# Constant products on TensorE in front of and between the first attention steps, and the exponentials' table load behind the second squares

## Chip, cores and metric

One Trainium2 chip; the kernel runs on one of its cores. The metric is the device time of one execution in microseconds (us). A profile is one execution recorded by the hardware profiler; times within it count from the first instruction.

## The reference

Two pre-norm layers over 8 sequences of 256 tokens with 256 channels, all float32. Layer 0 is an attention without separate query, key and value weights, then a mixture of 4 experts (2 per token) with a shared expert. Layer 1 is an RWKV recurrence, then a mixture of 8 experts. What the change touches is the attention of layer 0, on the normalised input `x`:

```python
w = (x @ W.T).reshape(Bb, Tt, HEAD, DIM_HEAD).transpose(0, 2, 1, 3)   # 16 heads of 16
q, k, v = _rms_norm(w, g1), _rms_norm(w, g2), _rms_norm(w, g3)
att = jnp.einsum('bhid,bhjd->bhij', q, k) / sqrt_d
score = jax.nn.softmax(att, axis=-1) + jax.nn.softmax(att, axis=-2)
y = jnp.einsum('bhij,bhjd->bihd', score, v).reshape(Bb, Tt, C)
return y @ W
```

## The kernel before

All eight sequences stay in SBUF as tiles `xs[b]` (128 partitions, two halves of 128 tokens). Before the first branch the kernel loads them, builds constants (`ident`, `ones` and others by GpSimd), sets the activation table for square roots with a one-element activation on the tile `spare` (L1476), and normalises and transposes sequence 0 in a PSUM pool `p0` (L223 to L252, tile `xmT`). Then it branches on a bound of the gains; the branch taken here calls `layers(True)`, whose attention is `attention_bounded`.

The attention is a list of small functions for each sequence, placed by number into steps (`steps`, with `at(n, f, ...)`). Within a step they run in the order of the list `mine`. For sequence 0 the order is: step 0 `norm` (already there) and `project_in`; step 1 `scale`; step 2 `turn`; from step 3 on four steps of `exponentials`, with `values` one step behind. For sequence 1: `ready` in step 0, `norm` and `project_in` in step 1, `scale` in step 4, `turn` in step 5; sequence 2 has its `norm` in step 5.

- `ready` is the layer norm (VectorE, with a power on GpSimd, L216 and L217); `norm` transposes it on TensorE (L246) and copies it out on ScalarE (L252).
- `project_in` multiplies by the weights (L499: 4 products of 256 columns, each recorded as two passes), squares on ScalarE (L504), sums over a head on VectorE (L506). Sequence 0 then takes a square root on ScalarE (L509), runs an `Exp` of one element to fetch the exponentials' table (L510) and inverts on VectorE (L511); the other sequences use a power on GpSimd (L515), about 5.4 us long.
- `scale` multiplies by that factor on VectorE (L525). `turn` transposes on TensorE (L539), copies `kT` out on ScalarE (L541), makes `qT` on VectorE (L544) and has GpSimd copy `nv` (L547).
- `exponentials` makes the scores (L563: four strips of 32 rows side by side, 512 columns, two passes each, into four PSUM tiles `sc`), takes the exponential on ScalarE (L576, L568), sums (L577) and divides (L579, L580). `values` multiplies by the values (L594).

TensorE's order is the order in which this program text issues (`tc.manual_schedule(engines={ENG.PE})`). The orders of the other engines' queues are laid out at compile time by a planner from priorities and estimated times; it also picks the PSUM buffer for each tile of a tag. The tag `ps` has 4 buffers, the tag `sc` 4. `tc.issue_after(i)` queues what is issued under it behind `i` on the same engine.

## Time and profile before

| | us |
|---|---|
| median of 3 runs (lowest, highest) | 754.26 (754.13, 755.09) |
| the profiled execution | 760.07 |
| its span, first to last instruction | 757.7 |
| TensorE matmul busy in the span | 653.3 (86%) |
| VectorE busy | 462.9 (61%) |
| ScalarE busy | 358.8 (47%) |
| GpSimd busy | 244.5 (32%) |
| mean granted TensorE clock | 0.941 |

How to read the lines of a profile: a row of the timeline begins with its start in us, then the time from the start of its first to the end of its last instruction, the engine (PE is TensorE, PEld its weight loads, DVE VectorE, ACT ScalarE, POOL GpSimd), the line of the kernel, the operation, the tile written and the tiles read, and xN for N instructions. The bracket gives the idle time of the engine before it and what ended that. PEclk is the granted TensorE clock, 1.00 for the full one.

### The profile page before, as it was taken

The page shows a single profiled execution, that of the slowest core. Times are in us where ns is not written, and L with a number is a line of the kernel's source. Part 1 is how long each engine was busy: PE and PEld are TensorE (multiplying, and loading weights), DVE is VectorE, ACT ScalarE, POOL GpSimd, SP SyncE. Part 2 cuts the span into 40 slices and gives each one's busy share as a digit, 9 for nine tenths or more (in the row PEclk, how much of TensorE's full clock was granted, in tenths as well). Part 3 has the DMA queues.
Part 4 walks back from the last instruction along what each step waited for, and adds up shares of the span by engine and source line. Part 5 has one row for each costly group of instructions (what it writes and reads, how often), then busy time and mean ns, then how long its engine had stood idle before and what let it go on. Part 6 is the DMA issues. An engine that isn't in the chain of part 4 may idle for free. (4 is left out here: it accounts for less than half of the span.)

```text
span 757.7 us, 10756 instructions
## 1 busy us (share of the span) xinstructions
PE 653.3 (86%) x3170; PEld 417.3 (55%) x3170; DVE 462.9 (61%) x1216; ACT 358.8 (47%) x761; POOL 244.5 (32%) x319
## 2 busy tenths in 40 slices
PE   3799999996989999998899888986848989989790
PEld 2355555555765666665566656654735656554460
DVE  6699878897351111110866877673998895745542
ACT  3588767772213233322377467544147464423230
POOL 3434333300212333323222132112141446465430
PEclk9699999998999999999999999998879999999996
DMA  7800000001101111112300010002780445556844
GB/s 227 292 1 15 15 15 15 15 15 48 65 15 33 52 36 42 43 41 85 118 29 27 28 39 11 28 29 72 231 283 8 138 126 170 172 194 220 269 127 143
DMA packets 38547, 66.85 MB, mean 88 GB/s; under 512 B 6006, under 2 KB 20654, under 8 KB 38480
## 3 DMA queue, kind: packets, MB, share of 16 engines
q1 hardware_dynamic: 30400, 47.01, 18.9%
q0 software_dynamic: 7392, 18.50, 7.9%
q8 instruction: 31, 0.51, 0.3%
q10 hardware_dynamic: 688, 0.55, 0.2%
q14 instruction: 36, 0.29, 0.1%
HBM read 51.32 MB, written 16.41 MB: 89 GB/s over the span
## 5 line engine op out<-in xcount | busy, mean ns | idle before, releaser
L1002 POOL DMA_INDIRECT xg<-asked,source x77 | 78.4, 1018 | 186.5 <-PE ps L1012 164.1
L1050 POOL DMA_INDIRECT back<-yg,row_i x77 | 80.6, 1047 | 113.7 <-ACT yg L1049 35.3
L1041 DVE TENSOR_TENSOR h<-h,mm 128x512 f32<-128x512 f32 x37 | 25.3, 685 | 108.3 <-PE mm L1020 108.2
L1014 ACT COPY hT<-ps 128x256 f32<-128x256 f32 (+1 forms) x77 | 36.4, 473 | 95.8 <-PE ps L1012 87.2
L1020 PE MATMUL mm<-v1s,xgT 128*128 x160 | 76.9, 600 | 1.5 <-ACT xgT L1014 0.8
L576 ACT ACTIVATE e<-sc,minus 128x512 f32<-128x512 f32 x96 | 59.9, 711 | 28.5 <-PE sc L563 28.4
L1020 PE MATMUL mm<-w2s,hT 128*128 x296 | 72.0, 382 | 0.0
L1020 PE MATMUL mm<-w1s,xgT 128*128 x148 | 71.6, 602 | 0.2 <-ACT xgT L1014 0.2
L1020 PE MATMUL mm<-w3s,xgT 128*128 x148 | 70.7, 597 | 0.0
L577 DVE TENSOR_REDUCE s<-e 128x2 f32<-128x512 f32 x96 | 60.5, 677 | 13.3 <-ACT e L576 13.1
L563 PE MATMUL sc<-qT,kT 32*128 32x512 f32 x256 | 58.1, 703 | 2.9 <-DVE qT L544 2.2
L1020 PEld LDWEIGHTS mm<-w2s,hT 128*128 128x128 f32 x296 | 53.7, 191 | 7.1 <-issue 1.4
L1170 PE MATMUL sc<-mix,rw 128*128 128x256 f32 x192 | 49.3, 405 | 5.9 <-DVE mix L1159 4.2
L515 POOL TENSOR_TENSOR rr<-rr,minus_half 128x32 f32<-128x32 f32 x7 | 38.0, 5429 | 50.0 <-DVE rr L513 49.9
L1012 PEld LDWEIGHTS ps<-ident,h 128*128 128x128 f32 x228 | 28.8, 141 | 44.0 <-issue 27.7
L1020 PE MATMUL mm<-v2s,hT 128*128 x160 | 44.3, 396 | 3.1 <-ACT hT L1014 3.1
L216 POOL TENSOR_TENSOR rs<-mv,eps_ln 128x2 f32<-128x2 f32 x40 | 8.6, 215 | 118.4 <-DVE mv L211 75.6
L1012 PE MATMUL ps<-ident,h 128*128 128x128 f32 x228 | 39.4, 276 | 8.4 <-DVE h L1035 7.2
L1020 PEld LDWEIGHTS mm<-w3s,xgT 128*128 128x128 f32 x148 | 28.0, 193 | 33.9 <-issue 33.2
L1170 PEld LDWEIGHTS sc<-mix,rw 128*128 128x128 f32 x192 | 38.2, 205 | 14.2 <-DVE mix L1159 5.3
L1039 ACT ACTIVATE h<-mm 128x512 f32<-128x512 f32 x37 | 22.1, 598 | 43.1 <-PE mm L1020 43.1
L1032 DVE TENSOR_TENSOR hb<-mm,bias 128x512 f32<-128x512 f32 x40 | 27.5, 687 | 22.5 <-PE mm L1020 18.9
(246 smaller groups left out, 1254.2 us busy)
## 6 DMA issues: line engine op xcount, KB each, us to landing
bias<-bd SPq DMA_DIRECT2D x40, 384.0 KB
y<-back SPq DMA_DIRECT2D x16, 512.0 KB
asked<-xm SPq DMA_DIRECT2D x16, 256.0 KB
x<-in_x_dram SPq DMA_DIRECT2D x8, 256.0 KB
w1s<-in_w_dram SPq DMA_DIRECT2D x4, 512.0 KB
w3s<-in_w_dram SPq DMA_DIRECT2D x4, 512.0 KB
w2s<-in_w_dram SPq DMA_DIRECT2D x4, 512.0 KB
v1s<-in_v1g_dram SPq DMA_DIRECT2D x8, 256.0 KB
```

Source lines behind the costliest of these rows:

```text
L515: on_pool["last"] = nc.gpsimd.tensor_tensor(rr, rr, half, ALU.pow)
L563: nc.tensor.matmul(pa, lhsT=q["kT"][rows, u, ts(t, P)], rhs=q["qT"][rows, u], start=True, stop=True)
L576: nc.scalar.activation(e, pa, AF.Exp, bias=minus)
L577: nc.vector.tensor_reduce(q["s"][:, t, h : h + 2], e, AX.X, ALU.add)
L1002: nc.gpsimd.indirect_dma_start(out=xgs[j], out_offset=None, in_=self.asked, in_offset=bass.IndirectOffsetOnAxis(ap=self.source[:, j : j + ...
L1012: nc.tensor.transpose(pt[:, c, :], src[:, ts(c, P)], ident)
L1014: nc.scalar.copy(to, pt)
L1020: nc.tensor.matmul(po.unsqueeze(1), lhsT=lhsT[:, c, :], rhs=w[:, ds(e, 1), c, :], start=(c == 0), stop=(c == n - 1))
L1032: nc.vector.tensor_tensor(hb, ph, biases[j][:, 0 : 2 * I2], ALU.add)
L1041: nc.vector.tensor_tensor(s, s, pg, ALU.mult)
L1050: inst = nc.gpsimd.indirect_dma_start(out=self.back, out_offset=bass.IndirectOffsetOnAxis(ap=self.row[:, j : j + 1], axis=0), in_=yg, in_o ...
L1170: last = nc.tensor.matmul(po[:, o, :], lhsT=w[:, c, ts(o, P)], rhs=m[:, c, :], start=(c == 0), stop=(c == NC - 1))
```

## The change

Four edits.

1. In front of the transposes of sequence 0, TensorE multiplies the 128x128 tile `ones` by itself 34 times, into a PSUM tile `idle` that nobody reads.
2. A new function `keep(n)` does n such products into a tile of the tag `ps`. It is the last in its step: 3 products at the end of step 0, 5 at the end of step 1, 9 at the end of step 2.
3. The one-element `Exp` on `spare` leaves sequence 0 and is issued in `project_in` of sequence 1, queued behind its squares on ScalarE.
4. `keep` is added to the list that orders a step.

```diff
             n = ap2.tile([P, TT, NH, DH], F32, tag="n", name="n")
-            nc.scalar.activation(n, pw4, AF.Square)
+            square = nc.scalar.activation(n, pw4, AF.Square)
+            if b == 1:
+
+                with tc.issue_after(square.ins):
+                    nc.scalar.activation(spare, eps_rms, AF.Exp)
             rr = ap2.tile([P, TT, NH], F32, tag="rr", name="rr")
             nc.vector.tensor_reduce(rr, n, AX.X, ALU.add)
             if b in turned_in:
 
                 nc.scalar.activation(rr, rr, AF.Sqrt, bias=eps_rms, scale=1.0 / DH)
-                nc.scalar.activation(spare, eps_rms, AF.Exp)
                 nc.vector.reciprocal(rr, rr)
...
+        def keep(n):
+
+            idle = fresh()[0]([P, P])
+            for _ in range(n):
+                nc.tensor.matmul(idle, lhsT=ones, rhs=ones, start=True, stop=True)
+
...
-            mine = (ready, norm, exponentials, scale, turn, project_in, to_tokens, values, turn_back, project_heads, take_norm, fill)
+            for n, k in enumerate((3, 5, 9)):
+                at(n, keep, k)
+            mine = (ready, norm, exponentials, scale, turn, project_in, to_tokens, values, turn_back, project_heads, take_norm, fill, keep)
...
     with tc.tile_pool(name="p0", bufs=1, space=PSUM) as p0:
+
+        idle = p0.tile([P, P], F32, tag="idle", name="idle")
+        for _ in range(34):
+            nc.tensor.matmul(idle, lhsT=ones, rhs=ones, start=True, stop=True)
         xn = layer_norm(lnp, 0, "xm", bufs=3)
```

## Prediction

> **What bounds the kernel now.** I read the page first, then the chain of waits, then the timeline of each engine over the first 48 us, then the windows of 1 us over the same stretch. The page says that TensorE is the busiest engine and where its clock is low:

> ```profile
> PE 653.3 (86%) x3170; PEld 417.3 (55%) x3170; DVE 462.9 (61%) x1216; ACT 358.8 (47%) x761; POOL 244.5 (32%) x319
> PEclk9699999998999999999999999998879999999996
> ```

> The chain that ended last covers only the last 17 us (moves to `back` and `y`), which the change doesn't touch. So the question is by how much the change brings forward the attention, and whether all behind it follows. It should: from 38 us on TensorE is busy without a hole in nearly every slice, and nothing later waits for a fixed time (the first weights have landed by 36 us, where the DMA share falls to 0). I take a shift at 35 us as a shift of the end, one to one.

> TensorE in the timeline:

> ```profile
> 10.16 1.23 PE L246 MATMUL ps<-ident,xm 128*128 128x128 f32 x4 [10.16 <-DVE xm L223]
> 12.77 3.34 PE L499 MATMUL ps<-awt,xmT 128*128 128x256 f32 x8
> 15.94 0.60 PE L246 MATMUL ps<-ident,xn 128*128 128x128 f32 x4
> 17.33 1.99 PE L499 MATMUL ps<-awt,xnT 128*128 128x256 f32 x8 [0.79 <-ACT xnT L252]
> 20.50 0.63 PE L539 MATMUL ps<-ident,n 128*128 128x128 f32 x4 [1.17 <-DVE n L525]
> 23.33 2.09 PE L563 MATMUL sc<-qT,kT 32*128 32x512 f32 x8 [2.21 <-DVE qT L544]
> 30.22 1.94 PE L594 MATMUL ps<-e,nv 128*32 128x256 f32 x16
> ...
> 42.46 1.14 PE L563 MATMUL sc<-qT,kT 32*128 32x512 f32 x8
> ```

> The same eight passes cost 3.34 and 1.99 us, the same four transposes 1.23 and 0.60, a free set of scores 2.09 and 1.14. The windows give the clock beside them (the first number after the stretch is its length, the next TensorE's busy time; the third from the right is the clock):

> ```profile
> 22.00:23.00 1.00, 0.00 (x0) 0.00 (x0) 1.00 (x2) 1.00 (x1) 1.00 (x1) 0.75 1.02 351
> 23.00:24.00 1.00, 0.67 (x4) 0.55 (x8) 0.19 (x1) 0.04 (x1) 1.00 (x1) 0.50 1.05 388
> 29.00:30.00 1.00, 1.00 (x3) 0.00 (x0) 1.00 (x2) 1.00 (x2) 0.00 (x0) 0.50 1.08 363
> 36.00:37.00 1.00, 1.00 (x18) 0.42 (x16) 1.00 (x3) 1.00 (x3) 0.00 (x0) 0.92 0.00 0
> ```

> It falls to half at 22.75 and rises at 36.1. ScalarE and VectorE between the squares of sequence 0 and its first exponential:

> ```profile
> 12.10 1.28 ACT L510 ACT_TABLE_LOAD   x1
> ...
> 17.29 1.28 ACT L509 ACT_TABLE_LOAD   x1
> 18.59 0.32 ACT L509 ACTIVATE rr<-rr,eps_rms 128x32 f32<-128x32 f32 x1
> 21.16 0.59 ACT L541 COPY kT<-ps 128x512 f32<-128x512 f32 x1 [1.20 <-PE ps L539]
> 21.76 1.28 ACT L576 ACT_TABLE_LOAD   x1
> 25.41 1.84 ACT L576 ACTIVATE e<-sc,minus 128x512 f32<-128x512 f32 x3 [2.36 <-PE sc L563]
> ...
> 16.84 0.68 DVE L506 TENSOR_REDUCE rr<-n 128x32 f32<-128x512 f32 x1
> 19.29 0.34 DVE L511 RECIPROCAL rr<-rr 128x32 f32<-128x32 f32 x1
> ```

> The `Exp` on `spare` runs at 12.10, long before the root, so the root's table is fetched again on the path (17.29), and the exponentials' at 21.76.

> **The 34 products.** No row shows such a product. It is two passes of 128 columns. From the second L499 and L246 rows, 1536 more columns cost 1.39 us, 0.12 us per 128: 0.23 a product at the full clock; at the low one a 256-column pass is 3.34 / 8 = 0.42. `ones` is ready at 1.1. In the trace the clock rose about 3.8 us after 12.1, where TensorE became steadily busy; I bound the rise at 4.5 to 8.1 and take 6. Then 4.9 / 0.42 = 11.7 products run slowly and 22.3 take 5.1 us: the end is 11.1 (10.5 to 12.1). They delay the first transposes, which could start at 10.16. From there: transposes 0.60, copy 0.59, eight passes 1.86, squares 0.60, with gaps about 14.9, against 16.80 now. But the sum over heads (L506) stands at 16.84 behind VectorE's layer-norm statistics of later sequences, which run without a hole from 14.28. If the planner leaves that order, the products give nothing here and cost nothing; the cover is 1.9 us (an end at about 13.0), past which a delay counts in full.

> **3 and 5 products.** Behind the first eight passes (end 14.2) 3 cost 0.7; the transposes of sequence 1 then run 14.9 to 15.5, its copy to 16.1, its eight passes to 18.1, its squares to 18.75 (now 19.96). The 5 run to 19.3, just when `turn` can start; beyond that each 0.23 would count. Queued behind both is only this TensorE work.

> **The tables.** The fetch at 17.29 goes, since the table set at 2.21 stays: the root starts at 17.55, not 18.59. L511 could follow at 17.95, but VectorE now holds 1.77 us of other work between L506 and L511, about the load and the root (1.28 + 0.32) which the planner seems to have filled. Without the load it should place L511 about 1.0 earlier (bounds 0, same order, and 1.3). `scale` ends at 19.3, `turn` runs to 19.95. On ScalarE the moved `Exp` stands behind the second squares: 18.75 + 1.28 + 0.20 = 20.25, and the copy of `kT` is queued behind it, so that the copy starts at 20.25, not 21.16: 0.9 earlier, 0.3 lost to the load. `qT` follows the copy and ends at 22.3 (now 23.19).

> **9 products.** 2.1 us behind `turn`, to 22.0, inside the wait for `qT`. They should hold the clock over 22.75, and the scores at 22.4 take 1.14 instead of 2.09. First exponential at 23.55 instead of 25.41: **1.86 earlier**, 0.9 by the table and 0.95 by the clock.

> **What is late next.** Two steps of exponentials are bound by ScalarE (25.41 to 31.35) and shift whole. TensorE then needs a score set's last strip, L594, L246 and the next scores before ScalarE goes on at 35.24. Between 26.1 and 30.2 the strips run singly, so a quarter of the array works: the windows show TensorE busy at 29.00 with the clock still at 0.50 after four such microseconds. So I expect that the full clock is lost again in the same strips (around 25 to 27.5), that the dense part behind them starts slow as now, and that the whole shifts by 1.9 to 2.3. I take 2.3, as the clock falls later than it did and so a little of that part is quicker. [...]

> [...]

> **Sum.** Profiled execution 760.07, minus 2.3 is 757.8. The median of the runs is 5.8 below the profiled one; the shift is taken over unscaled: 754.26 - 2.3 = 752.0.

> **Rivals.**

> [...]

> *VectorE's order stays.* L511 stays at 19.29 and the tables give nothing; only the 0.95 of the scores is left: 753.3.

> *PSUM buffers.* `keep` takes buffers of `ps`. Were the four handed out in turn, the 5 products would wait for `scale` (19.3) and `turn` start at 20.5 as now, and the first L594 would wait for the second `scale`, now 32.5, then 31.3, against its start at 30.22: 1.1 later, 755.4. Against it: between `project_in` and `scale` of a later sequence five tiles of `ps` are taken in TensorE's order, which would lock up if they went in turn; so free ones are picked.

> *The products run slowly* (ends slower). If a stream of 128-column products doesn't raise the clock, 34 x 0.42 = 14.3 us end at 15.4. Transposes, copy, eight slow passes, squares and sum then end at 22.6, not 17.5: 5.1 later, less the 1.0 of the root: 758.4. It decides from 0.35 us a product on, where the cover of 1.9 us is used up. The eight passes that raised it at 15.9 speak against it.

> *The table isn't where the text wants it* (slower). The `Exp` is tied only behind the second squares, not behind the root. If the planner puts those squares ahead of the root, both tables are fetched again: squares 18.75, `Exp` 20.25, load 1.28, root at 21.5 instead of 18.59; the inverse 2.6 later than 19.29, less 0.95: 755.9. Against it, the sum that the root needs is ready 1.2 before those squares can run.

> **Chances.** Shift as summed 0.45 (own range 750.8 to 753.4); clock holds 0.18; order stays 0.20; PSUM 0.07; slow products 0.06; table 0.04. 0.2% is 1.5 us, about what a measurement of this kernel can tell from no change. Faster by more: 0.36 of the first, all of the second, 0.06 of the third, 0.60. Within: 0.09, 0.14, 0.05, 0.28. Slower: the last two and 0.02 of PSUM, 0.12. The range runs from half a microsecond below the second case (748.8) to the PSUM case (755.4) and leaves out the two slow ones.

> **What would show it.** Right: two table loads before 30 us instead of four, none ahead of L509; L511 near 18.3; the first L563 row near 1.14 at about 22.4; the first exponential near 23.5; a clock below 1 somewhere from 25 to 33. Wrong: a first L246 beyond 13; L511 still at 19.3; a wait of the second group of products for `n`; a clock of 1.00 throughout (then 5 us, not 2.3).

## The result and the profile after

The changed kernel takes 752.03 us in the median of 14 runs (748.36 to 756.06); the kernel before took 755.28 beside it (14 runs, 748.06 to 763.12). The ratio is 0.9953, with a 95% interval of [0.9932, 0.9975]: by it 3.5 us less, between 1.9 and 5.1 (the medians differ by 3.25). Forecast were 752.0 us and 2.3 less, from a time before of 754.26, the median of the 3 runs known then. The profiled execution took 750.92 with a span of 748.8.

From the page after:

```profile
PE 658.8 (88%) x3272; PEld 425.5 (57%) x3272; DVE 462.4 (62%) x1216; ACT 356.1 (48%) x759; POOL 244.6 (33%) x319
PEclk9999997998999999999999999999888999999995
```

The 102 new TensorE passes are there (34 + 17 products, two passes each), ScalarE has two table loads fewer, and the low clock of the second slice is gone; one in the seventh is new. TensorE in the timeline after (the lines of the kernel have moved by a few):

```profile
1.14 9.70 PE L1493 MATMUL idle<-ones 128*128 128x128 f32 x68 [1.14 <-POOL ones L126]
12.35 1.89 PE L499 MATMUL ps<-awt,xmT 128*128 128x256 f32 x8
16.02 1.99 PE L499 MATMUL ps<-awt,xnT 128*128 128x256 f32 x8 [0.68 <-ACT xnT L252]
20.41 0.63 PE L542 MATMUL ps<-ident,n 128*128 128x128 f32 x4 [1.28 <-DVE n L528]
20.87 2.17 PE L646 MATMUL ps<-ones 128*128 128x128 f32 x18
23.24 1.14 PE L566 MATMUL sc<-qT,kT 32*128 32x512 f32 x8 [0.20 <-DVE qT L547]
28.23 1.07 PE L597 MATMUL ps<-e,nv 128*32 128x256 f32 x16
```

The 34 products end at 10.84, and the projections, scores and value products shown here run at the full clock. But `turn` (L542) starts at 20.41, against 20.50 before: it still waits for VectorE's `n`. Why, ScalarE and VectorE show:

```profile
14.36 0.60 ACT L504 ACTIVATE n<-ps 128x512 f32<-128x512 f32 x1 [2.47 <-PE ps L499]
18.66 0.32 ACT L513 ACTIVATE rr<-rr,eps_rms 128x32 f32<-128x32 f32 x1 [2.69 <-DVE rr L510]
19.48 1.28 ACT L508 ACT_TABLE_LOAD   x1
21.07 0.59 ACT L544 COPY kT<-ps 128x512 f32<-128x512 f32 x1
24.37 1.84 ACT L579 ACTIVATE e<-sc,minus 128x512 f32<-128x512 f32 x3 [2.72 <-PE sc L566]
30.98 1.84 ACT L579 ACTIVATE e<-sc,minus 128x512 f32<-128x512 f32 x3 [0.41 <-PE sc L566]
...
17.05 0.72 DVE L223 TENSOR_SCALAR xn<-x,mv,rs 128x256 f32<-128x256 f32 x2
17.97 0.65 DVE L510 TENSOR_REDUCE rr<-n 128x32 f32<-128x512 f32 x1
19.20 0.34 DVE L514 RECIPROCAL rr<-rr 128x32 f32<-128x32 f32 x1
```

The squares of sequence 0 are ready at 14.96 (before: 16.80), and no load stands ahead of the root any more. But the sum that the root needs, at 16.84 before, is now at 17.97, behind 1.1 us of other VectorE work (the two `xn` of sequence 2 among it), so the root starts at 18.66 (before: 18.59) and the inverse at 19.20 (19.29). The copy of `kT` gains 0.09. What is gained comes from the clock: 0.95 in the first scores (1.14 against 2.09), and 3.2 more by the third set of exponentials, 30.98 against 35.24.

### The profile page after: what moved, and what is told of

Its sections match the earlier page's. It is cut to its first block, busy times and chain, and to the rows that moved or that the text cites. A ratio compares the mean times of both kernels' runs of the same rounds, so it can differ in the third digit from the quotient of the medians.

```text
span 748.8 us, 10957 instructions
## 1 busy us (share of the span) xinstructions
PE 658.8 (88%) x3272; PEld 425.5 (57%) x3272; DVE 462.4 (62%) x1216; ACT 356.1 (48%) x759; POOL 244.6 (33%) x319
## 3 DMA queue, kind: packets, MB, share of 16 engines
q1 hardware_dynamic: 30400, 47.01, 19.1%
## 5 line engine op out<-in xcount | busy, mean ns | idle before, releaser
L580 DVE TENSOR_REDUCE s<-e 128x2 f32<-128x512 f32 x96 | 60.5, 677 | 14.3 <-ACT e L579 14.1
L1181 PEld LDWEIGHTS sc<-mix,rw 128*128 128x128 f32 x192 | 37.2, 201 | 14.2 <-DVE mix L1170 5.7
L1031 PE MATMUL mm<-v2s,hT 128*128 x160 | 42.3, 383 | 1.0 <-ACT xgT L1025 0.5
L1050 ACT ACTIVATE h<-mm 128x512 f32<-128x512 f32 x37 | 22.1, 598 | 42.3 <-PE mm L1031 42.2
L1031 PEld LDWEIGHTS mm<-v1s,xgT 128*128 128x128 f32 x160 | 27.3, 190 | 21.5 <-issue 18.4
## 6 DMA issues: line engine op xcount, KB each, us to landing
w2s<-in_w_dram SPq DMA_DIRECT2D x4, 512.0 KB, 10.2
```

The source lines that it names most:

```text
L580: nc.vector.tensor_reduce(q["s"][:, t, h : h + 2], e, AX.X, ALU.add)
L1031: nc.tensor.matmul(po.unsqueeze(1), lhsT=lhsT[:, c, :], rhs=w[:, ds(e, 1), c, :], start=(c == 0), stop=(c == n - 1))
L1050: nc.scalar.activation(s, pu, AF.Silu)
L1181: last = nc.tensor.matmul(po[:, o, :], lhsT=w[:, c, ts(o, P)], rhs=m[:, c, :], start=(c == 0), stop=(c == NC - 1))
```

## Experiments

Runs of one kernel differ by several us, and the profiles show the clock's low stretches elsewhere in each. So each theory is read from the start of named instructions in the profiles, and the ratios serve as a check. The start of the first, third and last (32nd) set of exponentials, of the copy of `kT`, and the low clock between 20 and 160 us:

| kernel | kT | first | third | last | low clock from 20 to 160 us, at | ratio to before |
|---|---|---|---|---|---|---|
| before | 21.16 | 25.41 | 35.24 | 169.79 | 22.5 (13.7 long), 104.4 (3.4) | 1 |
| whole change | 21.07 | 24.37 | 30.98 | 169.75 | 76.7 (3.4), 100.6 (3.4), 117.7 (10.2) | 0.9953 [0.9932, 0.9975] |
| after_again | 21.16 | 24.46 | 34.21 | 169.55 | 27.4 (6.8), 99.1, 123.0, 140.0 (3.4 each) | 0.9946 [0.9917, 0.9975] |
| table_alone | 21.24 | 25.50 | 35.32 | 173.03 | 21.9 (13.7), 100.4, 124.3 (3.4 each), 141.3 (10.2) | 1.0023 [0.9987, 1.0059] |
| products_alone | 21.11 | 24.41 | 31.01 | 170.17 | 43.8, 77.9, 101.8, 118.9, 142.8 (3.4 each), 159.9 | 0.9973 [0.9943, 1.0002] |
| nine_alone | 21.34 | 24.64 | 31.25 | 171.45 | 61.3, 78.4, 102.3 (3.4 each), 119.4 (10.2) | 0.9952 [0.9922, 0.9981] |
| no_front | 21.67 | 24.96 | 33.14 | 172.18 | 28.9, 63.0, 80.1, 104.0, 121.0, 144.9 (3.4 each) | 1.0001 [0.9967, 1.0034] |
| sum_first | 20.42 | 23.84 | 30.44 | 169.70 | 60.4, 77.4, 101.3, 118.4, 142.3 (3.4 each), 159.4 | 0.9953 [0.9923, 0.9982] |
| strip_fill_alone | 21.12 | 25.37 | 36.23 | 169.14 | 22.1 (13.7) | 0.9952 [0.992, 0.9983] |
| strip_fill | 20.40 | 23.81 | 30.42 | 163.53 | none | 0.988 [0.9836, 0.9925] |
| strip_fill_again (the kernel of strip_fill) | 21.16 | 24.57 | 34.02 | 168.50 | 27.8 (6.8), 79.0 (3.4) | 0.99 [0.9864, 0.9937] |
| nine_strip | 21.42 | 24.73 | 31.33 | 164.17 | none | 0.9907 [0.9873, 0.9942] |

**The whole change once more** (no edit).

> The changed kernel once more, for a second profile. Clock theory (the products keep the full clock from the first scores to the dense part at 28 to 35 us): the exponentials that began at 35.24 before and at 30.98 after begin near 31, with a clock of 1.00 from 23 to 36. Rival, the summed shift of the prediction (full clock only for the first scores, lost in the strips): near 33, with a clock of 0.50 somewhere from 25 to 33.

Here the clock fell, where the summed prediction had it. TensorE in this profile, and the windows of both profiles of the changed kernel, first the whole change's and then this one's:

```profile
25.20 4.06 PE L566 MATMUL sc<-qT,kT 32*128 32x512 f32 x8 [0.73 <-ACT e L579]
29.19 1.93 PE L597 MATMUL ps<-e,nv 128*32 128x256 f32 x16
32.10 2.09 PE L566 MATMUL sc<-qT,kT 32*128 32x512 f32 x8
```

```profile
23.90:27.30 3.40, 2.67 (x15) 1.00 (x8) 2.01 (x4) 2.93 (x8) 2.72 (x1) 1.00 1.06 376
27.30:30.70 3.40, 3.40 (x31) 1.32 (x30) 3.08 (x8) 3.06 (x8) 0.00 (x0) 1.00 1.07 372
```

```profile
23.90:27.30 3.40, 2.67 (x15) 0.91 (x7) 1.92 (x4) 2.84 (x8) 2.80 (x1) 1.00 1.06 369
27.30:30.70 3.40, 3.40 (x19) 0.98 (x18) 2.63 (x7) 2.67 (x7) 0.00 (x0) 0.51 1.07 371
```

With the same busy time in the same stretch the clock held once and fell once. The third set starts at 34.21, 1.03 earlier than before instead of 4.26. So both of the cases that the prediction kept apart occur, with one and the same kernel. Of the six profiles with the 9 products and no strip products (whole change, after_again, products_alone, nine_alone, no_front, sum_first) the clock held here in four and fell in two.

What differs between them can be read from the table. Within one profile the changes of the clock lie whole multiples of 3.41 us apart (the starts in the row of products_alone: 34.1, 23.9, 17.1, 23.9 and 17.1; the changes at 22.51, 36.16, 104.43 and 107.84 before: 13.65, 68.27 and 3.41), and where this grid lies against the program differs between the two executions of the changed kernel (falls at 76.7 and 27.4, 14.4 times 3.41 apart). The stretches above are windows of the grid of after_again; on that of the whole change's profile the windows run from 22.1 to 25.5 and from 25.5 to 28.9, so they cut the single strips (25.11 to 28.23) at another place. In all nine profiles with the 9 products (the six, and three below with strip products) the outcome goes with that place: the clock fell in the three where a window begins within 0.5 us of the first exponential, and held in the six where the nearest begins 0.87 to 1.65 us before it or 1.13 behind it.

**The table alone.**

```diff
-        for _ in range(34): ...          # the products in front
-            for n, k in enumerate((3, 5, 9)): at(n, keep, k)
```

> Only the moved Exp, none of the products. Clock theory: the table gives nothing, since the planner puts the sum over heads behind more of VectorE's statistics (its order for this kernel has the sum behind the two xn of sequence 2, two aggregates and one more statistic): root near 18.7, first scores at 23.2 to 23.6 taking 2.09, the third set of exponentials at 35 to 35.5, time within 1 us of before. Rival, the prediction's sum: 0.9 earlier at kT and everything behind it, the third set near 34.3, about 753.4 against 754.3.

The copy of `kT` starts at 21.24, the scores take 2.09, the third set starts at 35.32: nothing is gained, as the clock theory has it. VectorE in this kernel:

```profile
16.77 0.72 DVE L223 TENSOR_SCALAR xn<-x,mv,rs 128x256 f32<-128x256 f32 x2
18.30 0.67 DVE L510 TENSOR_REDUCE rr<-n 128x32 f32<-128x512 f32 x1
19.35 0.35 DVE L514 RECIPROCAL rr<-rr 128x32 f32<-128x32 f32 x1
```

The sum stands 1.46 later than before, behind more of the statistics: the move of the `Exp` is what puts it back, without a single product.

**The products alone.**

```diff
-            if b == 1:
-                with tc.issue_after(square.ins): nc.scalar.activation(spare, eps_rms, AF.Exp)
...
                 nc.scalar.activation(rr, rr, AF.Sqrt, bias=eps_rms, scale=1.0 / DH)
+                nc.scalar.activation(spare, eps_rms, AF.Exp)
```

> All products, but the Exp left where it was. Clock theory: as the whole change: table loads at about 12 and 17 us and again before the first exponential, first scores near 23.2 taking 1.14, first exponential near 24.4, third set near 31, time that of the whole change within 1 us. Rival, the prediction's sum: 0.9 later than the whole change at every step, with the third set 0.9 behind it.

```profile
16.57 1.28 ACT L509 ACT_TABLE_LOAD   x1
17.87 0.32 ACT L509 ACTIVATE rr<-rr,eps_rms 128x32 f32<-128x32 f32 x1
24.41 1.84 ACT L576 ACTIVATE e<-sc,minus 128x512 f32<-128x512 f32 x3 [1.42 <-PE sc L563]
```

With the old order (sum at 16.80) the load is back ahead of the root, and yet the first exponential starts at 24.41, within 0.04 of the whole change. The load had cover here: ScalarE fetches it at 16.57 while VectorE is at the sum, and the inverse stands at 19.23 behind VectorE's statistics in any case. Together with table_alone: at these starts the table edit is worth nothing and the products all of it. The ratio, 0.9973, doesn't tell this kernel from the whole change, nor quite from before.

**The 9 alone.**

```diff
-            for n, k in enumerate((3, 5, 9)):
-                at(n, keep, k)
+            at(2, keep, 9)
...                                        # and neither the 34 nor the moved Exp
```

> Only the 9 products behind the first turn, nothing else of the change. Theory (what counts is the clock held into the first scores; the 34, the 3 and the 5 stand where VectorE's queue sets the pace): root at 18.6, kT near 21.1, first scores near 23.3 taking 1.14, first exponential near 24.4, as with all products; the third set at 31 or, where the clock falls in the strips, near 34. Time between 751 and 755 beside 757 to 758 before. Rival (the 34 and the 5 are needed to keep the clock up): low clock at about 22.5 as before, scores taking 2.09, first exponential at 25.4, no gain.

Scores at 23.51 taking 1.14, first exponential 24.64, third set 31.25, ratio 0.9952: nine products carry the gain of the change within 0.3 us at these points. The first set of passes is slow again (3.62 us), which costs no more than that.

**All but the 34.**

```diff
-        for _ in range(34): ...          # the products in front; all else of the change stays
```

> The whole change without the 34 products. Theory: the first products of sequence 0 run slowly again (about 3 us), but the sum over heads stands behind VectorE's other work at about 18.0 and nothing behind it moves: kT near 21.1, first exponential 24.4, time that of the whole change within 1 us. Rival (the 34 bring the front forward): kT and all behind it about 1 later than with them.

Missed by both: 0.6 later at `kT` and at the first exponential, not 0 and not 1. TensorE's second passes start at 17.62 (whole change: 16.02), and behind them stand the second squares, the load and the one-element `Exp`:

```profile
19.65 0.60 ACT L504 ACTIVATE n<-ps 128x512 f32<-128x512 f32 x1 [0.65 <-PE ps L499]
20.27 1.28 ACT L508 ACT_TABLE_LOAD   x1
21.67 0.57 ACT L544 COPY kT<-ps 128x512 f32<-128x512 f32 x1
```

So the moved table makes the second squares part of the path, and the 34 products pay for that. Without the table's move (nine_alone) they aren't needed. The time, 1.0001, is above the whole change's; how much of that is the 0.6, and how much the fall at 28.9 in such executions, these runs can't part. It stays open why the time shows no gain over before, although the 9 products hold the clock through the first scores here too and the third set, at 33.14, is 2.1 earlier than before.

**The sum first.** The layer norms of sequences 2 to 7 are queued behind the sum over heads of sequence 0:

```diff
...
+            else:
+                with tc.issue_after(last["sum"].ins):
+                    seq[b] = dict(xn=layer_norm(ap2, b, "xn", bufs=1))
...
```

> The whole change, and the layer norms of sequences 2 to 7 queued on VectorE behind the sum over heads of sequence 0, so that the sum follows the squares at once. Clock theory with the order as what ate the table's gain: sum near 15.0, root near 15.8, the transposes of turn near 19.1 behind the 5 products instead of 20.4, the copy of kT near 20.2 behind the table load instead of 21.07, first exponential near 23.5 instead of 24.37, 0.9 less time than the whole change. Rival: the statistics pushed back now stand in front of qT, which starts no earlier than 21.7, and nothing is gained.

```profile
15.35 0.69 DVE L515 TENSOR_REDUCE rr<-n 128x32 f32<-128x512 f32 x1 [0.61 <-ACT n L509]
16.61 0.33 DVE L520 RECIPROCAL rr<-rr 128x32 f32<-128x32 f32 x1
21.16 1.39 DVE L551 TENSOR_SCALAR qT<-ps,gcol 128x512 f32<-128x512 f32 x2
```

With the order mended the inverse starts at 16.61, `turn` at 19.32, the copy of `kT` at 20.42 (0.65 earlier than in the whole change), first exponential 0.53 and third set 0.54 earlier. The direction and two thirds of the 0.9 are right; 0.1 went to statistics that now stand ahead of `qT`, and the copy itself waits for the load. In the time of the runs it doesn't show: the median is 755.87, beside 754.63 for the whole change in the same session (after_again), where 0.9 less was expected.

**Products in the strips.** They go into the second set of scores of every sequence, where TensorE waits for ScalarE strip by strip:

```diff
+                if (u, t) == (0, 1) and p < 2:
+                    if p == 0:
+                        idle = fresh()[0]([P, 2, T])
+                    strip = slice(STRIP * 3, STRIP * 4)
+                    nc.tensor.matmul(idle, lhsT=ones[strip, :], rhs=q["qT"][strip, u], start=True, stop=True)
```

In strip_fill this edit stands on top of sum_first, in strip_fill_alone on the kernel before.

> sum_first with two products of 512 columns on the fourth strip's 32 rows, in the second set of scores of every sequence, behind the first and the second strip, where that strip waits for ScalarE; their result is read by nobody. Theory (the clock falls where strips run singly, because a quarter of the array at work counts as a quarter; a window of 3.4 us needs about 0.4 of the array): the share in these windows goes from about 0.36 to 0.48, the low stretches between 22 and 155 us go, the sets of exponentials that took 5.6 or 7.4 us take 4.1, and the last set starts near 163 to 165 instead of 169.7; time 4 to 7 us under sum_first. Rival (the clock goes by idle gaps, not by the share of the array): low stretches stay, and the fourth strip is delayed by up to 0.5 a sequence: same time or up to 4 us more.

> The kernel before with nothing but those strip products. Theory: the clock is low when they first run (26 to 30 us), so that the first sequence gains nothing (third set at 35.2 or up to 1 later), but the later low stretches of the attention, each worth 0.5 to 3.3 us, go: last set near 165 to 167 instead of 169.8, time 3 to 5 us under before. Rival: low stretches stay, time as before or more.

The shares in the first of these are estimates of mine. By the count in the last section, 0.36 of the array was at work in the windows ahead of the falls at 104.4 before and at 76.7 and 100.6 in the whole change, and two products more are four passes of 0.43 us on a quarter of the array, 0.13 of a window of 3.41 us.

The windows of 20 us, of the whole change and then of strip_fill:

```profile
100.00:120.00 20.00, 19.07 (x142) 10.96 (x142) 16.12 (x39) 13.45 (x35) 6.29 (x4) 0.86 0.04 14
120.00:140.00 20.00, 19.07 (x126) 10.40 (x122) 13.65 (x34) 11.80 (x29) 4.09 (x6) 0.80 0.04 14
```

```profile
100.00:120.00 20.00, 18.85 (x161) 10.65 (x164) 16.98 (x43) 14.98 (x37) 7.18 (x5) 1.00 0.04 15
120.00:140.00 20.00, 18.84 (x163) 10.41 (x154) 16.33 (x41) 14.97 (x38) 7.19 (x5) 1.00 0.04 14
```

TensorE's busy time hardly differs, the clock does, and in the second stretch 163 passes get done instead of 126. On top of sum_first no low stretch is left between 20 and 160 us; the last set starts at 163.53, as expected. Alone, on the kernel before, the first low stretch stays and costs the first sequence 1.0 more, as expected, and the rest of the attention keeps the full clock; the last set, at 169.14, is later than the 165 to 167 expected, since the kernel before had only one more low stretch in that part of its profile, fewer than most, so that there was less to win than I had assumed.

strip_fill_again is the same kernel once more; nine_strip is the strip products with `at(2, keep, 9)` alone on the kernel before.

> The strip products on top of sum_first once more, since it was the fastest so far. Share theory: again no low stretch between 22 and 160 us, last set of exponentials near 163.5, about 1.2% under before. Rival (a lucky execution): low stretches of 3.4 us come back in the attention, each with 0.5 to 3.3 us, and the ratio goes to 0.995.

> The kernel before with only the 9 products behind the first turn and the strip products: no 34, 3 and 5, table and VectorE's order as before. Share theory: first exponential near 24.5, third set near 31.2, no low stretch to 160 us, last set near 164.3, time within 1 us of strip_fill. Rival (the 34 products, the table and the order of the sum carry part of strip_fill's gain): more than 2 us over strip_fill.

The repeat shows the limit: the clock fell again in the first strips (27.8) and once at 79.0, and the last set starts at 168.50, not near 163.5 as expected, so the strip products make a fall rarer and don't exclude it. The front varies too: the copy of `kT` is 0.76 later than in strip_fill, with the same code, so that the 0.65 of sum_first, seen in two profiles, isn't there in the third. The copy starts 9.23 to 9.24 us behind the end of the 34 products in all three profiles with the sum first (11.18, 11.17 and 11.93), and that end moves with the place at which the clock rises (5.8, 5.7 and 7.3). The time keeps its 1%: 0.99 and 0.988. nine_strip has the same without the 34, the 3, the 5, the table and the order: 746.63 us in the median, 746.55 for strip_fill_again in the same session, 754.91 for the kernel before. Both beat the kernel before; against the change they are some 0.5% ahead by the ratios to before, with intervals that overlap it a little, except for strip_fill, whose ratio rests on 6 runs. nine_strip is the simplest, with 9 products and two more per sequence.

## Why the prediction was right, and where not

The time came out as forecast, 752.0 against 752.03, and its parts did not. That the two agree so closely is luck: the term of the tables was too large, the one of the clock behind the first scores too small, and the difference of the medians, 0.95 larger than forecast (3.25 against 2.3), met a kernel before whose median was 1.02 higher in 14 runs (755.28) than in 3 (754.26). One of the prediction's own signs of being wrong came up, the inverse still at about 19.3 (19.20). In the profiled execution another did, a clock of 1.00 throughout (to 76.7); there two of the cases under the chances came true together in effect, as the clock held and the tables gave nothing.

- **The 34 products**: end 11.1 forecast (10.5 to 12.1), 10.84 measured; the clock rose at 5.02, where I had taken 6, and the bounds 4.5 to 8.1 were my estimate; that they are hidden by VectorE held for the root, but not for the second squares, which the moved table had put on the path. That step failed by 0.6 (no_front).
- **The tables**: 0.9 at `kT` forecast, 0.09 measured. The failing step is "Without the load it should place L511 about 1.0 earlier". The planner kept the inverse where it was and placed the sum 1.1 later (1.5 in table_alone, with no products at all). The rival "VectorE's order stays" named the right queue, and its 0.95 comes close to the 1.04 at the first exponential; the order itself did not stay, and the time that it gave, 753.3, left out what the clock gains behind. Why the planner does so was not tried.
- **The 9 products and the first scores**: 0.95 forecast (2.09 to 1.14), 0.95 measured, and 9 products alone give it. In the three profiles without them the clock fell at 21.9 to 22.5, in the nine with them it held there. (The prediction put the fall at 22.75; a mean of 0.75 from 22 to 23 means 22.50.)
- **What is late next**: forecast was that the clock falls again in the strips; it fell in two profiles of six and held in four. Where it fell in after_again, the third set gained 1.03, where it held 4.26. The chance for the rival that it holds was put at 0.18 against 0.45, by these six profiles too low. With the first exponentials 1.04 earlier and 3.2 more in four of six executions, an estimate of the mean is 1.04 + 4/6 x 3.2 = 3.2 us, beside the 3.5 measured. No run shows the 5 us that the forecast has for a clock that holds, to which the lower end of its range, 748.8, goes back: in the four profiles in which it held (whole change, products_alone, nine_alone, sum_first) the third set stands at 30.44 to 31.25, 3.99 to 4.80 earlier than before.
- **A shift at 35 us is a shift of the end**: this fits the mean of the runs but isn't shown, and for the pair of profiles it is wrong. The 4.26 of the profiled pair are gone at the last set (169.75 against 169.79), where the changed kernel's execution had met 13.7 us more low clock between 76 and 128; none of the profiles with the 9 products and no strip products is more than 0.24 earlier than before at that set. The spans' difference of 8.9 arises behind it, where the change edits nothing: from 175 us on the kernel before met 72 us of low clock in its profile, the changed one 60.
- **PSUM, slow products, lost table**: none occurred. The second group of products starts at 17.85, right behind the passes, and waits for no buffer; a product takes 0.22 us at the full clock (18 passes take 2.17 us, 10 take 1.28: 0.89 for 4 products more).
- **What goes ahead of a fall**: at 27.4 in after_again the clock fell after a stretch with TensorE busy for 2.67 of 3.40 us, and in the whole change it held after the same stretch with the same 2.67. The low stretches in the table are 3.4, 6.8, 10.2 and 13.7 us long.

## What to carry to other kernels

Here the clock fell at 100.6 in the whole change behind 3.40 of 3.40 us of busy TensorE, with 0.36 of the array at work (an estimate, see below); so look at the shape of the matmuls behind a long "busy", not at the busy time: two products a sequence in idle strips took 0.5% off the time by themselves (strip_fill_alone), as did nine in the wait ahead of the first scores (nine_alone). What the 34 in front are worth in time isn't settled; they moved the first exponential by 0.6 (no_front). An edit that takes a load off one engine can give nothing where the queue of the next one puts other work in the gap (table_alone); look at that queue before counting. And when executions differ by more than the effect, compare the starts of named instructions up to the first place where chance enters, not the spans. Here it enters with the place of the 3.41 us grid, which moves even the end of the 34 products (10.84 and 11.73 with the same code).

## What was not expected of the hardware

The clock fell even where TensorE is shown busy throughout, for 3.40 of 3.40 us ahead of the falls at 104.4 before and at 100.6 in the whole change, in passes that mostly use 32 of 128 rows (3.02 of the 3.40 us in both). The like stretch from 121.5 to 124.9 before, 3.40 of 3.40 us as well, kept the full clock. The profiles of all kernels without strip products have falls near 77 to 80, 99 to 104 or 118 to 124, some behind stretches with short gaps (2.54 of 3.40 us busy ahead of 117.7 in the whole change). With two products more on an unused strip, about 0.85 us of a quarter of the array each, the falls behind the first sequence were gone in three profiles of four, and the fourth has one, at 79.0.

One low stretch of 3.4 us cost a set of exponentials 1.5 us (5.63 instead of 4.10, at 103.22 before and at 99.39 in the whole change), less where it fell across two sets (3.57 and 4.05 instead of 3.09 and 4.10, from 76.41 in the whole change), and one of 10.2 us cost 3.3 (7.36, at 120.75 in the whole change).
